# Two cross-attention layers on one core: bias-key fetches, last value weights and one context mix put elsewhere

## The chip, the cores and the metric

The kernel runs on one core of one Trainium2 chip. The metric is the device time of one execution in microseconds (us). The kernel before takes 2015.84 us, the median of three runs (2015.71, 2015.84, 2021.12).

## The reference, cut to what matters

The input is x, 8 batches of 100 rows by 512, and a context ctx of 8 batches of 361 rows by 512. All arithmetic is in 32-bit floats. First comes a small attention with one head (called layer -1 here, its tiles have -1 in their names). Then come two big cross-attention layers l = 0, 1 with 16 heads of 128, and then a two-layer MLP with GELU:

```
h  = layer_norm(x);  q = h @ wq + bq            # per layer
k  = concat(ctx @ wk + bk, bias_k)              # one extra key per head
v  = concat(ctx @ wv + bv, bias_v)              # one extra value per head
x  = x + softmax(q k^T / sqrt(128)) v @ wo + bo
...
x  = x + gelu(layer_norm(x) @ w_fc1 + b_fc1) @ w_fc2 + b_fc2
```

The extra key bias_k needs a score of its own: for each head, a row E = sum over the head of wq * (bias_k - bk) / sqrt(128), which multiplies h. E for layer 1 is what the "bias keys" of this case are about.

## The kernel before, in words

Keys and values are never formed. A head's query is made 512 wide by multiplying with wk (`queries`, tile pq, then `wide_queries`, tile pqw, into the big SBUF array Z). It meets the transposed context cT to give scores (tiles sx, sz, sy, by Winograd's seven products in `pair_part`). The softmax weights are turned by 32x32 transposes on VectorE (`turned`, L358). The weights times ctx give a mixed context (`mixed`, tiles mx, mz, my, back into Z). A head's value weight wv then takes it to the 128 outputs (`head_out`, tile po, into O), and wo follows (`attn_out`, tile pwo).

**Steps and half steps.** A layer is done for four pairs of batches q = 0..3. A pair is done in three groups of rows g = 0..2 (`steps`), and a step has two half steps, one for each batch j of the pair. So a pair has six half steps, k = 2g + j = 0..5. In each half step the score units of that batch (nine or ten groups) are woven with a list `fill` of other units: projections of the next step (`ahead`), mixes of the half step before, head outputs of the step before, products with wo. The order is written out by hand; a list scheduler of the framework then fixes each engine's order from that order and its own estimate of times. Each engine runs its queue in order, and the SP queue, which issues nearly all DMAs, too.

**Closings.** wo is applied for two pairs of batches at once (half hf). Its last ten products, the sum with the rows of x, and the storing of the new rows are the "closing" (`close_units`). For q = 2 it is put into half steps k = 2 and 3 of the same layer; it is closing (0, 0) for layer 0. In k = 3 it fetches four sets of rows xr (`load_rows`, L370), adds to them (`back`, L990), and stores them again (`keep_rows`, L376). Still in k = 3, `rows_unit` fetches the two sets of rows that the next pair (q = 3) needs; they are normalised (L579) and transposed on TensorE (`normed`, ph, L582) at the beginning of k = 4.

**The buffers "h".** Rows fetched by `load_rows` lie in tiles with the tag "h", of which there are two. A fetched pair of bias-key pieces dk (`bias_fetched`, L596) lies in a tile of the same tag.

**The bias keys of layer 1.** There are eight pieces p = 0..7 (two heads each). Each has two units: a fetch (two broadcast DMAs on SP of 128 KB, together with the 512 KB weight tile wqe), and its sums (`bias_keys`: one subtraction on GpSimd, L620, then in `bias_sums` eight multiply-accumulates on VectorE, L603, each with a read of the accumulator; pinned to their place in VectorE's order). All are done in the six half steps of l = 0, q = 2. The fetch is joined to the unit in the middle of `fill`; the sums are put at its end. The pieces by half step k = 0..5 are: 0 / 1 / 2, 3 / 4 / 5 / 6, 7.

**The rings of weights.** `Ring` hands out weight tiles of 512 KB in the order in which units need them: ring "w" has six buffers (wq, wkT, wo, wqe, f1, f2), ring "v" has two (only wv). A new fetch is issued when units have used up earlier tiles.

**The end of layer 1.** For the last pair (l, q) = (1, 3) the head outputs of the first two groups are held back (`held`), and woven into the last step; the rest of them and the outputs of the last group come after the loop, with little score work beside them (`drain`).

**The mix.** In a half step with mixes, `lead` units of `part` (projections and head outputs) come before the first mix. A mix needs sums of columns, made on GpSimd (`column_sums`, L805 to L808) from the turned weights.

Of the kernel before, what the change touches and what calls it, by code (L numbers as in the profile page):

```python
# [19 lines left out]
DT = D // P  # L20
# [13 lines left out]
WHOLE = ((0, 5), (5, 10), (10, 16))  # L34
# [45 lines left out]
def two_cross_attentions(ctx: ExitStack, tc: tile.TileContext, a: dict, out: bass.AP):  # L80
# [11 lines left out]
    def psum(pool, shape, name):  # L92
        return pool.tile(shape, F32, tag=pool.name, name=name)
# [86 lines left out]
    def fill_cT(key, t):  # L180
# [3 lines left out]
    rings = {  # L184
        "ctx": Ring(cpool, [P, 20 * P], "ctx", C_SLOTS, fill_ctx),
        "ctx0": Ring(work, [P, 9 * GWIDTH // 2], "pT", 2, fill_ctx0),
        "cT": Ring(cpool, [P, 7, 2, KH], "cT", C_SLOTS, fill_cT),
        "w": Ring(wpool, [P, 1024], "w", W_SLOTS, fill_w),
        "v": Ring(vpool, [P, 1024], "v", V_SLOTS, fill_w),
    }  # L190
# [13 lines left out]
    def unit(fn, *keys):  # L204
        return fn, keys
# [406 lines left out]
    def bias_fetched(l, p):  # L612
        cols = slice(p * 2 * K, (p + 1) * 2 * K)
        dks[p] = dk = work.tile([P, 2, 2 * K], F32, tag="h", name=f"dk_{l}_{p}")
        broadcast(nc.sync, dk[:, 0, :], l, "bias_k", cols)
        broadcast(nc.sync, dk[:, 1, :], l, "bk", cols)

    def bias_keys(l, p):
        dk = dks.pop(p)
        nc.gpsimd.tensor_tensor(dk[:, 0, :], dk[:, 0, :], dk[:, 1, :], ALU.subtract)  # L620
        bias_sums(l, p, dk[:, 0, :], True)
# [259 lines left out]
            nc.sync.dma_start(out=t[:, j, : (h1 - h0) * L], in_=src.partition_broadcast(P))  # L881
        pbs[l, q] = t, h0

    def head_out(l, q, h):
        w = rings["v"].tiles["wv", l, q, h // 2].rearrange("p (c n) -> p c n", c=DT)
        t, h0 = pbs[l, q]
        add = t[:, :, (h - h0) * L : (h - h0 + 1) * L]
        nc.gpsimd.tensor_scalar(add, add, dv[:, l, h : h + 1], 1.0, ALU.mult, ALU.mult)
        ps = psum(ps_mm, [P, NQ], f"po_{l}_{q}_{h}")
        for c in range(DT):  # L890
            nc.tensor.matmul(  # L891
                ps,
                w[:, c, (h % 2) * K : (h % 2 + 1) * K],
                Z[:, c, :, h * L : (h + 1) * L],
                start=(c == 0),
                stop=(c == DT - 1),
            )
        nc.vector.scalar_tensor_tensor(
            O[:, h // 8, q % 2, h % 8, :].rearrange("p (b t) -> p b t", b=QB),
            ps.rearrange("p (b t) -> p b t", b=QB),  # L900
            vec[f"bv{l + 1}"][:, h : h + 1],
            add,
            ALU.add,
            ALU.add,
        )
# [216 lines left out]
    steps = [(l, q, g) for l in range(2) for q in range(B // QB) for g in range(NG)]  # L1122
# [4 lines left out]
    def e_units(l):  # L1127

        ks = [(W, ("wqe", l, p)) for p in range(H // 2)]
        return [(unit(lambda p=p: bias_fetched(l, p), ks[p]), unit(lambda p=p: bias_keys(l, p), ks[p])) for p in range(H // 2)]  # L1130

    def project_units(n):
        l, q, g = steps[n]
        res = []
        if g == 0:
            res += [unit(lambda c=c: normed(l, q, c)) for c in range(DT)]
            res.append(unit(lambda: bias_scores(l, q)))
        later = None
        h0, h1 = HEADS[g]
        ready = next(h for h in range(H) if (h + 1) * L >= PAIRS[g][0] + 2 * P)  # L1140
        for h in range(h0, h1):
            if q == 0 and h % 2 == 0:
                if later:
                    res += later
                    later = None
                key = "wkT", l, 0, h // 2
                res.append(unit(lambda p=h // 2: wk_transposed(l, p), (W, ("wkr", l, h // 2)), (W, key)))
            res.append(unit(lambda h=h: queries(l, q, h), (W, ("wq", l, q, h // 2))))
            if later:
                res += later  # L1150
            later = [unit(lambda h=h: wide_queries(l, q, h), (W, ("wkT", l, q, h // 2)))]
            if h == ready:
                later.append(unit(lambda: pair_sums(l, q, 0, PAIRS[g][0])))
        return res + later

    def mix_units(n, j):
        l, q, g = steps[n]
        return [
            unit(lambda m=m, part=part: mixed(l, q, g, j, m, part), ("ctx", ("ctx", l, q * QB + j)))
            for m in range(2)  # L1160
            for part in range(4)
        ]

    def out_units(n):
        l, q, g = steps[n]
        res = [unit(lambda h=h: head_out(l, q, h), ("v", ("wv", l, q, h // 2))) for h in range(*WHOLE[g])]
        return [unit(lambda: None)] + res

    def probs_unit(n):
# [22 lines left out]
    def product_units(l, hf, *names):  # L1192
        return [
            unit(lambda cp=cp, name=name: attn_out(l, hf, cp, name), (W, ("wo", l, hf, cp, PRODUCTS[name][0])))
            for name in names
            for cp in range(2)
        ]

    def close_units(l, hf):
        res = [unit(lambda: out_sums(0))]  # L1200
        res += product_units(l, hf, "P3") + [unit(lambda: out_sums(1))] + product_units(l, hf, "P5", "P6", "P7")
        tags = ("h", "h", "hT", "p") if (l, hf) == (1, 1) else ("h",) * 4
        fetch = [unit(lambda b=b, t=t: load_rows(b, t)) for b, t in zip(range(hf * 4, hf * 4 + 4), tags)]
        last = [
            unit(lambda j=j: back(ys[l, hf], j * L, hf * 4 + j, keep_rows)) for j in range(4)
        ]
        if (l, hf) == (1, 1):
            return fetch + res + product_units(l, hf, "P4") + last
        return res + fetch[:2] + product_units(l, hf, "P4") + last[:1] + fetch[2:3] + last[1:2] + fetch[3:] + last[2:]
# [75 lines left out]
    for n, (l, q, g) in enumerate(steps):  # L1285
        ahead = project_units(n + 1) if n + 1 < len(steps) else []
        half_ahead = (len(ahead) + 1) // 2
        for j in range(QB):
            fill = []
            k = 2 * g + j  # L1290
            if q % 2 == 0 and (l or q):
                closing = close_units(*((l, q // 2 - 1) if q else (l - 1, 1)))
                fill += {2: closing[:9], 3: closing[9:]}.get(k, [])
            elif q % 2:
                fill += {(4 if l and q == 3 else 0): product_units(l, q // 2, "P1"), (5 if l and q == 3 else 2): product_units(l, q // 2, "P2")}.get(k, [])
            mix = mix_units(n, 0) if j else mix_units(n - 1, 1) if n else []
            part = ahead[:half_ahead] if j == 0 else ahead[half_ahead:]
            outs = []
            if n == len(steps) - 1:
                outs = held[:4] if j == 0 else held[4:8]  # L1300
            elif j and n:
                outs = out_units(n - 1)
                if n == len(steps) - 2:
                    held, outs = outs + [probs_unit(n)] + out_units(n)[1:], []
            part = woven(part, outs) if len(part) > len(outs) else woven(outs, part)
            if mix:
                lead = (len(part) + 2) // 3 if ahead else len(part) - 2 + j
                fill += part[:lead]
                part = part[lead:]
                fill += woven(part, mix) if len(part) > len(mix) else woven(mix, part)  # L1310
            else:
                fill += part
            if l == 0 and q == 2:
                for fetch, sums_ in e_units(1)[4 * k // 3 : 4 * (k + 1) // 3]:
                    at = len(fill) // 2
                    fill[at] = both_of(fill[at], fetch)
                    fill.append(sums_)
            if l == 0 and q % 2:
                fill = woven(fill, sums_part(q // 2, k))
            if n and j == 0 and n < len(steps) - 1:  # L1320
                (fn, keys), (early, _) = fill[len(fill) * 3 // 4], probs_unit(n - 1)
                fill[len(fill) * 3 // 4] = unit(lambda fn=fn, early=early: [fn(), early()], *keys)
            if g == 1 and j and n < len(steps) - 2:
                at = len(fill) * 3 // 4
                fill[at] = both_of(fill[at], rows_unit((q + 1) % 4))
            groups = score_units(n, j)
            k = 0
            for i, us in enumerate(groups):
                units += us
                upto = (i + 1) * len(fill) // len(groups)  # L1330
                units += fill[k:upto]
                k = upto
    n = len(steps) - 1
# [38 lines left out]
```

## Time and profile before

| | |
|---|---|
| three runs | 2015.71, 2015.84, 2021.12 us |
| the profiled execution | 2018.84 us |
| its span, first to last instruction | 2017.0 us |
| TensorE (PE) busy | 1963.9 us, 97% of the span |
| VectorE (DVE) busy | 1276.8 us, 63% |
| ScalarE (ACT) busy | 757.4 us, 38% |
| GpSimd (POOL) busy | 707.2 us, 35% |
| mean granted TensorE clock | 0.997 |

PE is matmul, PEld the loading of weights into TensorE. A line of the timeline has start, length, engine, line of the kernel, operation, tiles (out<-in), shape and count; the bracket at the end is the engine's idle time just before it and what ended that. Times are from the start of the span.

### The profile page before, as it was taken

Reading aid. Unit: us, or ns where it says so; the run is one execution under the profiler, and the core shown is the slowest. Engines: PE = TensorE matmul, PEld = TensorE weight load, DVE = VectorE, ACT = ScalarE, POOL = GpSimd, SP = SyncE. Lnnn points to the kernel's source line nnn. Section 1 sums busy time; section 2 is a strip of 40 time slices with the busy share of each in tenths; the row PEclk is TensorE's granted clock in tenths of the full one; section 3 lists DMA queues with packets and bytes.
Section 4 is the critical chain, followed back from the end, with each engine's and each line's share of the span. In section 5 each row is a group of like instructions: output and inputs, shape, how many; then the busy total and the mean of one; then the engine's idle time right before and its main releaser. Section 6 shows DMA issues by size and latency. Waiting matters only on the chain.

```text
span 2017.0 us, 31494 instructions
## 1 busy us (share of the span) xinstructions
PE 1963.9 (97%) x10991; PEld 1814.2 (90%) x10991; DVE 1276.8 (63%) x3523; ACT 757.4 (38%) x2002; POOL 707.2 (35%) x1147
## 2 busy tenths in 40 slices
PE   9989999999999999999999999999999999999998
PEld 5668899999999889999999898999998998889998
DVE  2554776667676767666775766676766667765543
ACT  0324544444443343444433344444433444421231
POOL 3223432543345144425243323333243243225140
PEclk9999999999999999999999999999999999999999
DMA  7686224642544446625534453234244442135342
GB/s 252 254 305 218 85 82 141 215 136 76 188 141 138 136 140 207 200 66 176 172 119 128 113 180 102 87 93 158 88 125 125 136 124 79 53 107 168 117 127 73
DMA packets 250682, 283.89 MB, mean 141 GB/s; under 512 B 37608, under 2 KB 212108, under 8 KB 247196
## 3 DMA queue, kind: packets, MB, share of 16 engines
q1 hardware_dynamic: 246340, 271.51, 42.9%
q0 software_dynamic: 2112, 6.40, 0.9%
q10 hardware_dynamic: 2072, 3.97, 0.6%
q8 instruction: 88, 1.44, 0.3%
q14 instruction: 70, 0.57, 0.1%
HBM read 242.86 MB, written 38.97 MB: 140 GB/s over the span
## 4 chain that ended last, share of the span: by engine, by line
PE 79%; DVE 10%; DMA 4%; ACT 3%; issue 2%; POOL 1%; SPq 0%; DVEq 0%; ACTq 0%; POOLq 0%
PE sx L731 9%; PE mx L841 9%; PE mz L841 7%; PE pq L671 7%; PE pqw L687 7%; PE po L891 7%; PE pwo_P L954 6%; DVE pT L358 5%; PE sz L731 5%; PE my L841 3%; PE sc L478 2%; PE sy L731 2%; PE pfx L1094 2%; PE pgx L1045 2%; DMA xr<-xd 1%
## 5 line engine op out<-in xcount | busy, mean ns | idle before, releaser
L358 DVE STREAM_TRANSPOSE pT<-p 32x192 f32<-32x192 f32 (+1 forms) x1664 | 602.1, 362 | 84.3 <-ACT p L342 54.5
L841 PE MATMUL mx<-pT,ctx 128*128 128x256 f32 (+3 forms) x960 | 281.3, 391 | 11.2 <-DVE Z L867 6.6
L731 PE MATMUL sx<-cT,Z 128*128 128x181 f32 x1152 | 229.6, 318 | 3.2 <-DVE p L771 3.1
L841 PE MATMUL mz<-pT,ctx 105*128 105x256 f32 (+3 forms) x768 | 208.3, 393 | 7.3 <-POOL pT L805 4.9
L731 PEld LDWEIGHTS sx<-cT,Z 128*128 128x128 f32 x1152 | 195.2, 191 | 16.6 <-DVE p L771 5.2
L765 POOL TENSOR_SCALAR p<-nsb 128x1 f32<-128x1 f32 x192 | 39.1, 223 | 477.6 <-DVE pT L358 421.4
L841 PEld LDWEIGHTS mx<-pT,ctx 128*128 128x128 f32 (+1 forms) x960 | 170.0, 190 | 30.6 <-DVE Z L867 6.8
L891 PE MATMUL po<-Z,wv 128*128 128x200 f32 x1024 | 194.6, 334 | 1.4 <-DMA wv<-in_L_xattn_wv_dram 1.4
L687 PE MATMUL pqw<-q,wkT 128*128 128x200 f32 x1024 | 194.2, 332 | 0.0
L671 PE MATMUL pq<-hT,wq 128*128 128x200 f32 x1024 | 192.4, 332 | 0.0
L785 ACT ACTIVATE p<-p,nm 128x362 f32<-128x362 f32 x192 | 114.8, 598 | 178.2 <-DVE nm L784 172.5
L891 PEld LDWEIGHTS po<-Z,wv 128*128 128x128 f32 x1024 | 176.4, 191 | 5.6 <-DMA wv<-in_L_xattn_wv_dram 2.0
L841 PEld LDWEIGHTS mz<-pT,ctx 128*128 128x128 f32 (+1 forms) x768 | 144.0, 191 | 40.9 <-ACT Z L853 8.1
L687 PEld LDWEIGHTS pqw<-q,wkT 128*128 128x128 f32 x1024 | 176.2, 189 | 4.8
L671 PEld LDWEIGHTS pq<-hT,wq 128*128 128x128 f32 x1024 | 175.3, 189 | 2.9
L784 DVE TENSOR_REDUCE nm<-p 128x1 f32<-128x362 f32 x192 | 101.6, 529 | 103.6 <-ACT p L776 93.2
L714 POOL TENSOR_TENSOR sums<-Z 128x256 f32<-128x256 f32 x96 | 70.7, 737 | 234.1 <-ACT Z L690 145.4
L690 ACT COPY Z<-pqw 128x400 f32<-128x400 f32 x256 | 122.9, 490 | 73.6 <-PE pqw L687 73.5
L731 PE MATMUL sz<-cT,sums 128*128 128x181 f32 x768 | 149.3, 316 | 0.7 <-ACT p L759 0.7
L342 ACT ACTIVATE p<-p,rden 128x362 f32<-128x362 f32 (+2 forms) x216 | 129.1, 599 | 32.0 <-DVE rden L341 32.0
L731 PEld LDWEIGHTS sz<-cT,sums 128*128 128x128 f32 x768 | 124.8, 189 | 1.0 <-ACT p L759 1.0
L841 PE MATMUL my<-pT,ctx 128*128 128x256 f32 (+3 forms) x384 | 102.5, 388 | 0.0
(380 smaller groups left out, 3123.2 us busy)
## 6 DMA issues: line engine op xcount, KB each, us to landing
wv<-in_L_xattn_wv_dram SPq DMA_DIRECT2D x64, 512.0 KB
wq<-in_L_xattn_wq_dram SPq DMA_DIRECT2D x64, 512.0 KB
wkT<-wkd SPq DMA_DIRECT2D x48, 512.0 KB
cT<-cTd SPq DMA_DIRECT2D x16, 1267.0 KB
wo_S<-wod SPq DMA_DIRECT2D x32, 512.0 KB
f<-in_L_xattn_w_fc_dram SPq DMA_DIRECT2D x32, 512.0 KB
wo_A<-in_L_xattn_wo_dram SPq DMA_DIRECT2D x24, 512.0 KB
xr<-xd SPq DMA_DIRECT2D x45, 200.0 KB
```

Source lines behind the costliest of these rows:

```text
L342: nc.scalar.mul(p[:rows, :n], p[:rows, :n], rden[:rows])
L358: nc.vector.transpose(dst[keys, :, :, i, :], src[i * QD : (i + 1) * QD, :, :, quarter, :])
L671: nc.tensor.matmul(ps, w[:, c, (h % 2) * K : (h % 2 + 1) * K], hTs[l, q][:, c, :], start=(c == 0), stop=(c == DT - 1),)
L687: nc.tensor.matmul(ps[:, c, :], w[:, h % 2, cc * P : (cc + 1) * P], qs[h], start=True, stop=True)
L690: nc.scalar.copy(Z[:, 2 * c2 : 2 * c2 + 2, :, h * L : (h + 1) * L], ps.rearrange("p c (b t) -> p c b t", b=QB),)
L714: nc.gpsimd.tensor_tensor(t[:, 0], a2[:, :2, :], a2[:, 2:, :], ALU.add)
L731: nc.tensor.matmul(ps[:, :KH], st["a"][a][:, c, :], st["ct"][:, blk, c, :], start=(first and c == 0), stop=(c == 1), skip_group_check=not ...
L784: nc.vector.tensor_reduce(nm, p[:, :S1], AX.X, ALU.max, negate=True)
L785: nc.scalar.activation(p[:, :S1], p[:, :S1], AF.Exp, bias=nm, accum_out=den)
L841: nc.tensor.matmul(ps, cx[:w, blk, :], pT[:w, u, :], start=first, stop=last, skip_group_check=more)
L891: nc.tensor.matmul(ps, w[:, c, (h % 2) * K : (h % 2 + 1) * K], Z[:, c, :, h * L : (h + 1) * L], start=(c == 0), stop=(c == DT - 1),)
L954: nc.tensor.matmul(ps, w[:, h, :], OB[i, j][:, h, :], start=(h == 0 and not more), stop=(h == 7), skip_group_check=more)
```

## The change

There are three independent edits.

1. The pieces of the bias keys by half step become 0, 1 / 2, 3 / none / none / 4, 5 / 6, 7. Half steps k = 2 and 3, those with the closing, have none. Each fetch still stands near the middle of `fill`, and each sum at its end.
2. For (l, q) = (1, 3), heads 8 to 15 (four weight tiles wv) take their tile from ring "w" in place of ring "v". In the order of ring "w" these four stand after the last pair's four tiles for products P1 and P2, and before the closing's tiles.
3. In the last step but one, (1, 3, 1), second half step (j = 1), `lead` is larger by one: the mixes begin one unit of `part` later. `part` there is four units: a `pair_sums` (GpSimd), queries of head 15, wide queries of heads 14 and 15. Two stood before the mixes, and one each after four and after eight mixes; now three stand before, and one after all eight.

```diff
-    def head_out(l, q, h):
-        w = rings["v"].tiles["wv", l, q, h // 2].rearrange("p (c n) -> p c n", c=DT)
+    def head_out(l, q, h, ring="v"):
+        w = rings[ring].tiles["wv", l, q, h // 2].rearrange("p (c n) -> p c n", c=DT)
...
     def out_units(n):
         l, q, g = steps[n]
-        res = [unit(lambda h=h: head_out(l, q, h), ("v", ("wv", l, q, h // 2))) for h in range(*WHOLE[g])]
+        def ring(h):
+            return "w" if (l, q) == (1, 3) and h >= 8 else "v"
+
+        res = [
+            unit(lambda h=h: head_out(l, q, h, ring(h)), (ring(h), ("wv", l, q, h // 2))) for h in range(*WHOLE[g])
+        ]
         return [unit(lambda: None)] + res
...
             if mix:
-                lead = (len(part) + 2) // 3 if ahead else len(part) - 2 + j
+                lead = (len(part) + 2) // 3 + (n == len(steps) - 2 and j) if ahead else len(part) - 2 + j
...
             if l == 0 and q == 2:
-                for fetch, sums_ in e_units(1)[4 * k // 3 : 4 * (k + 1) // 3]:
+                for fetch, sums_ in e_units(1)[slice(*{0: (0, 2), 1: (2, 4), 4: (4, 6), 5: (6, 8)}.get(k, (0, 0)))]:
                     at = len(fill) // 2
                     fill[at] = both_of(fill[at], fetch)
                     fill.append(sums_)
```

## The prediction, made before the result was known

> **What bounds the kernel now.** I read the page's first and fourth parts, then TensorE's waits, then a table by stretches around the largest ones, then the timeline.
>
> ```profile
> PE 1963.9 (97%) x10991; PEld 1814.2 (90%) x10991; DVE 1276.8 (63%) x3523; ACT 757.4 (38%) x2002; POOL 707.2 (35%) x1147
> PE 79%; DVE 10%; DMA 4%; ACT 3%; issue 2%; POOL 1%; SPq 0%; DVEq 0%; ACTq 0%; POOLq 0%
> ```
>
> TensorE sets the end. No edit removes work from it, so only its waits can give time. Over the whole span those listed sum to 47.1 us, in 55 waits. Its waits in the half steps of l = 0, q = 2 (560 to 790 us), and then from 1700 to 1850 us:
>
> ```profile
> PE ph L582 <- DVE xr L579: 4.0, 1, 4.0
> PE mx L841 <- DVE Z L867: 2.1, 1, 2.1
> PE sx L731 <- ACT p L756: 1.3, 1, 1.3
> ...
> PE mz L841 <- POOL pT L805: 1.6, 2, 1.0
> PE po L891 <- DMA wv<-in_L_xattn_wv_dram: 1.4, 2, 0.7
> ```
>
> The two largest cost more than they show. Stretches (PE, PEld, DVE, ACT, POOL busy; PE clock; DMA):
>
> ```profile
> 690.05:692.10 2.05, 0.00 (x0) 0.03 (x1) 1.95 (x6) 0.00 (x0) 0.23 (x1) 1.00 0.57 168
> 692.10:696.00 3.90, 3.90 (x12) 3.61 (x13) 3.71 (x10) 0.37 (x1) 1.11 (x3) 0.56 0.31 107
> 708.88:712.86 3.98, 0.01 (x1) 0.00 (x0) 3.18 (x9) 0.37 (x1) 2.02 (x5) 1.00 0.62 204
> 712.86:717.00 4.14, 4.13 (x16) 3.77 (x17) 1.83 (x5) 0.37 (x1) 4.06 (x7) 0.59 0.58 169
> ```
>
> After each wait the clock falls: 3.90 x (1 - 0.56) = 1.72 us and 4.14 x (1 - 0.59) = 1.70 us of matmul time lost. No smaller wait after 150 us has this. So the pair costs 2.06 + 1.72 = 3.78 and 3.98 + 1.70 = 5.68 us, 9.46 together. Why the second is there:
>
> ```profile
> 686.82 0.36 SPq L596 DMA_DIRECT2D dk<-in_L_xattn_bias_k_dram  x1
> 689.52 0.30 SPq L370 DMA_DIRECT2D xr<-xd  x1
> ...
> 708.05 0.80 DVE L603 SCALAR_TENSOR_TENSOR wqe<-wqe,dk 128x128 f32<-128x128 f32 x1
> 708.93 0.31 SPq L370 DMA_DIRECT2D xr<-xd  x1
> 712.27 0.55 DVE L579 TENSOR_SCALAR xr<-xr,mv,rstd 100x512 f32<-100x512 f32 x1 [0.69 <-DVE pT L358]
> 712.87 0.70 PE L582 MATMUL ph<-ident,xr 100*128 100x100 f32 x3 [3.98 <-DVE xr L579]
> ```
>
> The closing frees one "h" buffer at 686.8; piece 4 of the bias keys takes it. The next goes at 689.5 to the first rows of pair q = 3. The second rows must wait until piece 4's last sum ends at 708.85; their fetch goes out at 708.93, and TensorE waits for them.
>
> **What the Trainium skill says.** "TensorE: Matmul & The Clock Gate", Part 1: the clock halves after an idle window of about 3.4 us, a free-running one. The trace agrees on the half and on the length, but shows it after a wait of 2.06 us, so here the trace decides. "SBUF — State Buffer", Who interferes with whom: a VectorE instruction with two SBUF inputs blocks against a GpSimd one that reads SBUF. The trace agrees: one L603 takes 0.28 us mostly, 0.80 at 708.05, while GpSimd runs L717.
>
> **Edit 1, removed.** With no piece in k = 2 and 3, the buffers freed at 686.8 and 689.5 go to the two rows of q = 3. A rows fetch at 680.05 served its reader at 683.08, so they are there by 693, and needed at 708.9. The wait for ph goes, with its clock loss: **-5.68**. VectorE also loses 3.3 us (665.66 to 669.13, pieces 2 and 3) and 3.4 us (piece 4) in these half steps. The other wait, mx on L867, is less sure. VectorE stood 2.72 us for the closing's third rows (683.08) since these await the store of the first ones; that chain stays. The same closings without bias keys, in layer 1, show 2.48 us (q = 0) and 2.56 us (q = 2) of TensorE waits in k = 2 and 3, and no clock loss. Against 9.46 that is 6.9 to 7.0 less. So I take **-1.3** for the second wait, of -3.78 to 0.
>
> **Edit 1, added.** Fetches (two dk DMAs, 0.33 to 0.78 us of SP each, and one wqe) and GpSimd's 0.73 us stay eight each. In k = 1 the fetch of piece 3 stands in SP's queue for a buffer that piece 1's sums free, as piece 2's did at 588.34; in k = 4 the two fetches meet the same release by ph as two do now at 718.56. On VectorE k = 0, 1 and 4 end with 16 sums for 8. Eight took 1.78 us at 741.78. Behind the end of k = 0 stand three transposes, GpSimd's L805 at 588.70 and a mz whose weight load already waits 0.27 us for it: no slack, so 0 to 1.9 us; other projections can stand before it in the new order, and I take **+0.8**. After k = 1 the closing's O-sums (L934) end at 627.9 and are needed at 631.4: 3.5 us of cover hide 1.8. If the cover were gone, 1.8. After k = 4 VectorE's L771 ends at 746.1 for a matmul at 750.2: hidden likewise. The 1.27 us at 786.08, where 16 sums stood ahead of the lone tile's L331, stay: k = 5 has two pieces in both kernels. Two wqe tiles at once leave four of ring "w". The fetches of wqe at 731.80 and 739.87 follow the ends of other tiles' last matmuls (pq at 731.6, pqw at 739.7), so a fetch takes any free buffer, and none waits for a pinned sum with less than 10 us to its use: nothing. Edit 1: -5.68 - 1.3 + 0.8 = **-6.2**.
>
> **Edit 2.** Fetches of wv at 1793.42 and 1814.09, each issued when two heads had ended, met matmuls at 1796.79 and 1817.42: 3.3 us of landing against 2.7 us of two heads.
>
> ```profile
> 1814.09 0.38 SPq L156 DMA_DIRECT2D wv<-in_L_xattn_wv_dram  x1
> 1817.42 1.62 PE L891 MATMUL po<-Z,wv 128*128 128x200 f32 x8 [0.66 <-DMA wv<-in_L_xattn_wv_dram]
> 1801.58 1.13 PE L841 MATMUL mz<-pT,ctx 128*128 128x256 f32 x4 [0.67 <-POOL pT L805]
> ```
>
> In ring "w" the four come out a half step or more ahead: both waits go, 0.66 + 0.70. But behind the first (heads 8, 9) stands mz at 1801.58, waiting for L805; L805 hangs on VectorE's transposes, which did not wait for TensorE there, so its 0.67 grows to 1.37 and that gain is given back. I take **-0.7** of -1.36 to -0.66. Four S1 and S2 tiles of the closing now follow heads 9 to 15. The last is issued about 1820, used about 1834, and lands in 3.3 us: nothing; were it late, some 1 us.
>
> **Edit 3.** At 1714.33 mz waits 0.98 us for L805, and mx 0.25 for L806 next. One wide query (8 matmuls, 1.35 us, as pqw at 1706.24) before them covers both; no DMA moves. It no longer stands after four mixes, where it was cover: **-0.9** of -1.2 to 0.
>
> **Sum:** -6.2 - 0.7 - 0.9 = -7.8. On the profiled execution: span 2017.0 - 7.8 = 2009.2, with its 1.84 around it 2011.0. That execution is 3.0 above the median of the runs; from the median, 2015.84 - 7.8 = **2008.0**.
>
> **Rivals.** (a) The wait moves on: without ph's wait VectorE, 3.18 of 3.98 us busy in it, has no time to catch up, mx on L867 stays with its clock loss, and k = 1 pays its 1.9. For: it ran 9 instructions there. Against: it has 3.4 us less to do just before. -5.68 + 1.9 - 1.6 = -5.4, with half of the ph gain given back -2.5: about 2013. (b) The list order changes after 560 us wherever two instructions were nearly equal, and the waits from there on, 23.2 us without the two large ones, come out otherwise. For: the same half step k = 5 of different pairs shows none or 1.27 us. Against: the units after q = 2 are unchanged. If they grow by a sixth, 3.9, it is 2012; if instead all uncertain terms end at their best, -5.68 - 3.78 - 1.36 - 1.2 = -12.0, 2003.8. (c) Slower: the doubled blocks of sums. At 777.00 a block of 16 took 5.6 us, as GpSimd ran beside it, and stopped L331. If each of the three new ones costs TensorE the 5.6 - 1.8 = 3.8 us and then the clock, 1.7, that is 3 x 5.5 = 16.5, less 5.68 + 1.3 + 1.6: +7.9, about 2024. It decides from about 2 us each, where the clock falls: 3 x 3.7 = 11 against 8.6. Against it: the block of 16 at 665.66 took 3.3 us and no wait followed.
>
> **How the numbers follow.** Forecast 0.66 (own range 2005 to 2011), (a) 0.17, (b) 0.11, (c) 0.06. Two in ten left out gives 2003.5 to 2015. A measurement of this kernel can tell about 0.3%, 6.0 us: faster means below 2009.8. The forecast lies 1.8 under it with about 2 us of spread, so 0.56 of its 0.66 is faster; with 0.05 of (b), 0.61. Slower 0.05 of (c). The rest, 0.34, is the same.
>
> **What would show it.** Right: TensorE's wait for ph gone, no clock loss near 690 to 715; both rows fetches of q = 3 within 3 us of each other; no dk issue in k = 2, 3; no wait of po on wv; mz's wait at the last step but one gone, and a longer one of mz in the drain. Wrong: a new wait of mz or sx at the start of k = 1, a mx wait over 2 us with the clock at half, or a wait on a weight of ring "w".

## The result, and the profile after

The changed kernel takes 2009.66 us, the median of six runs (2007.22 to 2010.5), beside 2017.92 us for the kernel before on the same chip (six runs, 2015.22 to 2021.18). The ratio is 0.9959, with a 95% interval of 0.9947 to 0.9971: 8.3 us less. The profiled execution took 2009.43 us, its span is 2007.7 us; before, 2018.84 and 2017.0.

The page of the kernel after, its first and its fourth part:

```profile
PE 1959.0 (98%) x10991; PEld 1811.7 (90%) x10991; DVE 1277.3 (64%) x3523; ACT 757.0 (38%) x2002; POOL 707.6 (35%) x1147
PE 78%; DVE 12%; ACT 4%; DMA 2%; issue 2%; POOL 1%; SPq 0%; DVEq 0%; ACTq 0%; POOLq 0%
```

The counts of instructions are those of before; TensorE is busy 4.9 us less although it does the same work. That is for the most part the clock: the two falls of before were 3.4 us of it. The waits are 43.0 us in all, where they were 47.1. TensorE's waits of the kernel after, first in the stretch 560 to 790 us, then in 1700 to 1850 us (total, count, longest):

```profile
PE mz L841 <- POOL pT L805: 1.8, 1, 1.8
PE mx L841 <- ACT Z L850: 1.6, 1, 1.6
PE pwo_P L954 <- issue: 1.6, 1, 1.6
PE sx L731 <- ACT p L756: 1.3, 1, 1.3
...
PE mz L841 <- POOL pT L805: 1.6, 1, 1.6
PE mx L841 <- DVE Z L867: 1.4, 1, 1.4
PE sx L731 <- DVE p L771: 1.1, 2, 0.7
```

The 4.0 us of ph and the 2.1 us of mx on L867 are gone. Three waits of 1.6 to 1.8 us stand there that the kernel before did not have. In the second stretch the two waits of po for a DMA are gone, and one wait of mz has grown. In the same stretch as before, the timeline of the kernel after around the rows of the next pair:

```profile
688.45 3.08 SPq L370 DMA_DIRECT2D xr<-xd  x2
...
709.00 0.51 PE L582 MATMUL ph<-ident,xr 100*128 100x100 f32 x4
709.35 0.81 PE L731 MATMUL sx<-cT,sums 128*128 128x181 f32 x4
```

Both rows fetches go out together, 20 us ahead of ph, and ph has no idle time before it. The stretches after the three new waits, in the columns of before (PE, PEld, DVE, ACT, POOL busy; PE clock; DMA):

```profile
591.42:595.40 3.98, 3.98 (x22) 3.71 (x23) 3.29 (x14) 1.87 (x6) 3.98 (x6) 1.00 0.97 295
634.95:639.00 4.05, 4.05 (x24) 4.05 (x25) 2.78 (x10) 1.60 (x4) 2.06 (x3) 1.00 0.90 291
699.57:703.60 4.03, 3.73 (x18) 3.18 (x19) 2.54 (x8) 2.76 (x7) 0.00 (x0) 1.00 0.00 0
```

No clock is lost in these stretches: 1.00 where before had 0.56 and 0.59.

**The two new waits of k = 1.** At its start, in the timeline of the kernel after:

```profile
586.21 0.29 DVE L603 SCALAR_TENSOR_TENSOR wqe<-wqe,dk 128x128 f32<-128x128 f32 x1
...
589.73 0.75 DVE L358 STREAM_TRANSPOSE pT<-p 32x192 f32<-32x192 f32 x2
...
590.57 0.79 POOL L805 TENSOR_TENSOR pT<-pT 128x288 f32<-128x288 f32 x1 [3.80 <-DVE pT L358]
...
591.42 1.24 PE L841 MATMUL mz<-pT,ctx 128*128 128x288 f32 x4 [1.78 <-POOL pT L805]
```

The block of 16 sums stands before the last two transposes; they release GpSimd's L805, and that releases mz. At the end of k = 1:

```profile
617.05 1.83 DVE L930 TENSOR_TENSOR O<-O 128x1600 f32<-128x1600 f32 x1
618.79 5.34 DVE L358 STREAM_TRANSPOSE pT<-p 32x192 f32<-32x192 f32 x14
624.16 1.82 DVE L603 SCALAR_TENSOR_TENSOR wqe<-wqe,dk 128x128 f32<-128x128 f32 x1
...
633.03 1.82 DVE L934 TENSOR_TENSOR O<-O 128x1600 f32<-128x1600 f32 x1
...
622.28 3.56 POOL L932 TENSOR_TENSOR O<-O 128x1600 f32<-128x1600 f32 x1
...
634.95 2.27 PE L954 MATMUL pwo_P<-O,wo_S 128*128 128x200 f32 x12 [1.55 <-issue]
```

The first sum lasts 1.82 us in place of 0.28: it ends at 625.98, just after GpSimd's L932 (625.84). Four more take 0.80 to 0.82 us while GpSimd makes its `pair_sums` (L714 to L717). The block lasts 7.1 us (624.16 to 631.28), L934 follows it and comes too late. "issue" as a releaser means that the profile shows none; L934 ends at 634.85 and the matmul starts at 634.95.

**Where the time went, by stage.** The stage borders are the first sy matmuls of half steps in the timeline: of k = 5 of (l, q) = (0, 1), of (0, 3), of (1, 0), and of k = 3 of (1, 3). Microseconds from border to border, the last one to the end of the span:

| profile of | (0,1) k = 5 and q = 2 | q = 3 | layer 1 up to (1,3) k = 3 | the end |
|---|---|---|---|---|
| before | 265.3 | 196.4 | 726.4 | 304.9 |
| after | 261.7 | 196.1 | 724.2 | 301.7 |
| edit 1 alone | 261.4 | 196.3 | 723.9 | 303.8 |
| edit 2 alone | 264.3 | 196.0 | 725.2 | 303.0 |
| edit 3 alone | 266.7 | 196.4 | 726.5 | 303.3 |
| piece 4 alone moved | 260.3 | 196.3 | 724.3 | 304.6 |
| the same, with idle sums in k = 3 | 264.9 | 196.3 | 726.4 | 304.9 |
| the same, with the buffer held in k = 3 | 265.0 | 196.3 | 724.3 | 305.4 |
| pieces 1, 2, 3 alone earlier | 268.2 | 196.1 | 725.1 | 304.3 |
| piece 4, edits 2 and 3 | 258.8 | 195.8 | 726.3 | 301.8 |
| the same again | 261.0 | 196.1 | 726.3 | 302.3 |
| after again | 261.5 | 196.4 | 724.3 | 301.5 |

Edit 1 acts in the first column (-3.6), edits 2 and 3 in the last (-3.2). In the first column several kernels have the same order of instructions on PE, DVE, ACT and POOL, and so are further executions of one program: before and runs 2 and 3 take 265.3, 264.3 and 266.7 us, the changed kernel, run 1 and the repeat 261.7, 261.4 and 261.5. The difference of the means is 3.9 us.

The -2.2 of layer 1 can't be put down to an edit. From 760 us until edit 3 acts at 1713 us the order of instructions on these four engines is the same before and after. TensorE's waits there sum to 10.2 us before and 8.4 after, in two executions of one order, and the column runs from 723.9 to 726.5 over all these kernels.

### The profile page after: what moved, and what is told of

Its sections match the earlier page's. It is cut to its first block, busy times and chain, and to the rows that moved or that the text cites. A ratio compares the mean times of both kernels' runs of the same rounds, so it can differ in the third digit from the quotient of the medians.

```text
span 2007.7 us, 31493 instructions
## 1 busy us (share of the span) xinstructions
PE 1959.0 (98%) x10991; PEld 1811.7 (90%) x10991; DVE 1277.3 (64%) x3523; ACT 757.0 (38%) x2002; POOL 707.6 (35%) x1147
## 4 chain that ended last, share of the span: by engine, by line
PE 78%; DVE 12%; ACT 4%; DMA 2%; issue 2%; POOL 1%; SPq 0%; DVEq 0%; ACTq 0%; POOLq 0%
PE sx L731 9%; PE mx L841 9%; PE mz L841 7%; PE pq L671 7%; PE po L891 7%; PE pqw L687 7%; PE pwo_P L954 7%; DVE pT L358 6%; PE sz L731 5%; PE my L841 3%; PE sy L731 2%; PE pfx L1094 2%; PE sc L478 2%; PE pgx L1045 2%; ACT p L342 1%
## 5 line engine op out<-in xcount | busy, mean ns | idle before, releaser
L714 POOL TENSOR_TENSOR sums<-Z 128x256 f32<-128x256 f32 x96 | 70.7, 736 | 223.4 <-ACT Z L690 134.8
```

The source lines that it names most:

```text
L714: nc.gpsimd.tensor_tensor(t[:, 0], a2[:, :2, :], a2[:, 2:, :], ALU.add)
```

## The experiments

Each time is against the kernel before on the same chip, as a ratio with its 95% interval; 0.001 is 2.0 us.

**1. The first edit alone.**

```diff
-                for fetch, sums_ in e_units(1)[4 * k // 3 : 4 * (k + 1) // 3]:
+                for fetch, sums_ in e_units(1)[slice(*{0: (0, 2), 1: (2, 4), 4: (4, 6), 5: (6, 8)}.get(k, (0, 0)))]:
```

> Edit 1 alone. Theory A (a piece of bias keys held the buffer that the rows of q = 3 needed; the clock loss goes with the wait): ph's wait and both clock losses gone, mx wait after the closing about 1.6 us as in the closings of layer 1, and the two new waits of the changed kernel (mz on L805 at the start of k = 1, 1.8 us; the third product of the closing in k = 2 on VectorE's L934, 1.6 us) there too: -3.7 us up to the start of q = 3, -4 to -5 in all. Rival B (all of the change's gain is edit 1's, and the rest of the trace's difference chance): -8.

Measured: 0.998 (0.9972 to 0.9987), -4.0 us. Its waits in 560 to 790 us are those of the whole change: mz 1.77, pwo 1.56, mx on L850 1.57, sx 1.3 us, no ph. So edit 1 gave about half of the gain.

**2. The second edit alone** (heads 8 to 15 of the last pair through ring "w").

```diff
+            return "w" if (l, q) == (1, 3) and h >= 8 else "v"
```

> Edit 2 alone. Theory (given back): both waits of po on wv gone (0.70 and 0.66), but the wait of mz on L805 in the drain grows from 0.67 to about 1.4, so -0.7 us. Rival (nothing given back): mz's wait stays at 0.67, -1.4. Rival (ring w now late): a wait of pwo on a weight in the closing, 0 or slower.

Measured: 0.9987 (0.9976 to 0.9997), -2.6 us, and 1.8 us less in the last stage. In its timeline from 1790 to 1822 us one wait of TensorE is left:

```profile
1795.89 1.13 PE L841 MATMUL mz<-pT,ctx 128*128 128x256 f32 x4 [1.65 <-POOL pT L805]
```

Both po waits went, and mz, which stood behind the first, waits 1.65 in place of 0.67 us: a gain of 0.66 + 0.70 is partly given back, as the prediction had it. The order of the matmuls is that of before, so the two traces can be laid over each other, matmul by matmul. The two po bring 0.9 us each, mz takes 0.9 back, and 1.1 us is left at the end of the span. The other 0.7 of the 1.8 us is a wait of sx for L771 at 1774.05 (0.58 us), ahead of all this, which runs 1, 3 and 4, without edit 2, don't have either: it is scatter of the execution before.

**3. The third edit alone.**

```diff
-                lead = (len(part) + 2) // 3 if ahead else len(part) - 2 + j
+                lead = (len(part) + 2) // 3 + (n == len(steps) - 2 and j) if ahead else len(part) - 2 + j
```

> Edit 3 alone. Theory: mz's wait of 0.98 on L805 and mx's 0.25 in (1,3,1) j = 1 gone, a wait of sx on L771 of about 0.7 a few us later in place, as in the changed kernel: -0.5 to -0.8. Rival (full gain): no new wait, -1.2.

Measured: 0.9992 (0.9983 to 1.0001), -1.6 us: no clear difference by itself. In its timeline from 1700 to 1730 us mz's 0.98 and mx's 0.25 are gone, and one wait has come:

```profile
1725.51 0.88 PE L731 MATMUL sx<-cT,Z 128*128 128x181 f32 x4 [0.69 <-DVE p L771]
```

1.23 less 0.69 is 0.5 us of waits. The sums of the three single edits, -4.0 - 2.6 - 1.6 = -8.2 us, agree with -8.3 for the whole, but each has an interval of 1.5 to 2.2 us to either side, so that an agreement within 0.1 us is chance.

**4. Which piece matters: piece 4 alone moved**, from k = 3 to k = 4. Pieces 1 to 3 stay.

```diff
+                for fetch, sums_ in e_units(1)[slice(*{0: (0, 1), 1: (1, 2), 2: (2, 4), 4: (4, 6), 5: (6, 8)}.get(k, (0, 0)))]:
```

> Of edit 1 only piece 4 is moved (pieces 0 / 1 / 2,3 / none / 4,5 / 6,7); k = 0, 1 and 2 as before, edits 2 and 3 not made. Theory A (the buffer): ph's wait with its clock loss gone, no new waits at the starts of k = 1 and in k = 2: at least -5.7 us, and more than edit 1 alone. If the mx wait on L867 in k = 3 came from VectorE's 16 sums at the end of k = 2, it stays (2.1 us and clock loss) and the gain ends at -5.7; if it came from piece 4, it falls to about 1.6 and the gain is about -7.9. Rival (VectorE's relief in k = 2 and 3): a third of the sums moved, -1 to -2.

Measured: 0.9966 (0.9954 to 0.9978), -6.9 us. TensorE's waits in 560 to 790 us:

```profile
PE mx L841 <- DVE Z L867: 2.2, 1, 2.2
PE sx L731 <- ACT p L756: 1.3, 1, 1.3
PE mz L841 <- ACT Z L853: 0.3, 1, 0.3
```

ph's wait is gone, the two of k = 1 do not arise, and mx on L867 stays, with its clock (0.57 in the 3.93 us after it). The whole gain of edit 1 is in this one piece. But piece 4 takes two things out of k = 3: a tile with the tag h, and eight sums from VectorE. The next runs put back one at a time.

**5. Piece 4 moved, and eight idle sums put in its place in k = 3.** They work on zeros and take no tile h.

```diff
+    def idle_sums():
+        zero = ef[:, 2 * DT * H :]
+        for _ in range(8):
+            tc.keep_in_program_order(
+                nc.vector.scalar_tensor_tensor(
+                    zero, zero, 1.0, ident[:, : P - H], ALU.mult, ALU.mult, accum_out=junk_sum
+                )
+            )
...
+            if (l, q, k) == (0, 2, 3):
+                fill.append(unit(idle_sums))
```

> As the run with only piece 4 moved, but with a block of eight idle sums of nearly the same shape (112 columns, zeros times the identity, written back over zeros) left at the end of k = 3 on VectorE, where piece 4's sums stood. Only the buffer is freed, VectorE has the same load there. Theory A (the buffer): ph's wait stays gone, and the time is that of piece 4 alone within 1.5 us: about -6. Rival (VectorE's relief): a wait of ph or of a mix near the start of k = 4 comes back, -2 or less.

Measured: 0.9996 (0.9986 to 1.0005): the gain is gone although the rows are there in time. Lines of this kernel are 11 higher: L816 is L805. Its timeline at the end of k = 3:

```profile
687.99 2.71 SPq L370 DMA_DIRECT2D xr<-xd  x2
...
707.17 0.27 DVE L616 SCALAR_TENSOR_TENSOR E<-E,ident 128x112 f32<-128x112 f32 x1
...
711.87 0.37 DVE L358 STREAM_TRANSPOSE pT<-p 32x192 f32<-32x192 f32 x1
...
712.33 0.81 POOL L816 TENSOR_TENSOR pT<-pT 128x256 f32<-128x256 f32 x1 [0.29 <-DVE pT L358]
...
713.18 1.13 PE L852 MATMUL mz<-pT,ctx 128*128 128x256 f32 x4 [2.34 <-POOL pT L816]
```

Here the sums alternate with the last seven transposes, and these end at 712.24. GpSimd's column sums come after them, and mz after those: 2.34 us, and the clock falls (0.62 over the next 4.02 us). So the sums alone are enough to make TensorE wait, by another chain than the one that the kernel before showed. The order is not quite that of before: there the eight sums stood as a block ahead of the seven transposes.

**6. Piece 4 moved, the tile h held in k = 3 but only one multiply-accumulate.** It was run to see whether the buffer alone would be enough too.

```diff
+    def held_fetch():
+        bias_fetched(1, 4)
+        dks["held"] = dks.pop(4)
+
+    def held_sum():
+        dk = dks.pop("held")
+        half = dk[:, 0, :K]
+        tc.keep_in_program_order(
+            nc.vector.scalar_tensor_tensor(
+                half, half, 1.0, dk[:, 1, :K], ALU.mult, ALU.mult, accum_out=junk_sum
+            )
+        )
...
+            if (l, q, k) == (0, 2, 3):
+                at = len(fill) // 2
+                fill[at] = both_of(fill[at], unit(held_fetch))
+                fill.append(unit(held_sum))
```

> Piece 4 as in the run with piece 4 alone moved (its sums in k = 4); but in k = 3 a tile of the tag h still takes the two rows of bias keys at the old place, and one multiply-accumulate (0.3 us of VectorE) at the old place of the sums lets it go. The output is the reference's. Theory A, the held buffer alone makes TensorE wait: the buffer comes free near 706, the second rows' fetch follows it, 3.9 us from issue to ph as in the kernel before, so ph is ready near 709.9 where it is wanted near 708.5: a wait of 1 to 2 us for ph, none of mz for L805, 2 to 4 us slower than with piece 4 moved. Theory B, the eight sums on VectorE in front of the last transposes alone: nothing of it is seen, the waits of the run with piece 4 moved, -7 us against before. Theory C, the eight sums delay both the release of the buffer and the transposes: the wait for ph is there but short, 0.5 to 2 us, and the 2.34 us of mz seen with idle sums is not; the two runs together give what before showed as one wait.

Measured: 0.9996 (0.9986 to 1.0006), 5.5 us slower than with piece 4 moved. Its timeline:

```profile
705.29 0.31 SPq L370 DMA_DIRECT2D xr<-xd  x1
...
709.01 1.07 DVE L579 TENSOR_SCALAR xr<-xr,mv,rstd 100x512 f32<-100x512 f32 x1 [1.38 <-DMA xr<-xd]
...
710.14 0.59 PE L582 MATMUL ph<-ident,xr 100*128 100x100 f32 x2 [2.95 <-DVE xr L579]
```

The buffer comes free at 704.9, after the one sum, and the second rows are still late: 4.85 us from issue to ph, which is wanted at 707.2. All three theories had the size wrong. A, a wait of 1 to 2 us, is nearest; it is 2.95 us, with a fall of the clock after it. B falls, and so does C's short wait.

Runs 5 and 6 together are the answer to why the kernel before waited. Two chains ended within about a microsecond of each other: buffer, rows, L579, ph; and sums, transposes, L805, mz. In its own trace both are seen:

```profile
708.89 2.69 DVE L358 STREAM_TRANSPOSE pT<-p 32x192 f32<-32x192 f32 x7
711.67 0.72 POOL L805 TENSOR_TENSOR pT<-pT 128x256 f32<-128x256 f32 x1 [0.44 <-DVE pT L358]
713.37 1.96 PE L841 MATMUL mz<-pT,ctx 128*128 128x256 f32 x4
```

L805, which mz needs, ended at 712.39; ph began at 712.87, and mz came right behind it. Only the later chain was listed. Each alone costs nearly all of it (5.6 and 5.5 us over run 4 by the medians, 2016.19 and 2016.13 to 2010.6), and taking either away gains next to nothing. Moving the piece took both away.

**7. The early half of edit 1 alone:** pieces 1, 2 and 3 go to k = 0 and 1, piece 4 stays.

```diff
+                for fetch, sums_ in e_units(1)[slice(*{0: (0, 2), 1: (2, 4), 3: (4, 5), 4: (5, 6), 5: (6, 8)}.get(k, (0, 0)))]:
```

> The other half of the first edit alone: pieces 1, then 2 and 3 go to k = 0 and k = 1 as in the change, piece 4 stays in k = 3. Theory A, the doubled blocks cost what the run with the whole first edit showed over the one with piece 4 alone: a new wait of mz for L805 of about 1.8 us at the start of k = 1 and one of pwo for L934 of about 1.5 us at the end of k = 1, the 3.98 of ph stays: 1 to 3.3 us slower than before, ratio 1.0005 to 1.0016. Rival, the fetches and the closing's chain set the end of k = 3 anyway, so that earlier waits are taken up there: ratio 1.000, the ph wait shorter by what was lost earlier.

Measured: 1.0006 (0.9999 to 1.0013), +1.2 us, and 2.9 us more in the first stage. Its waits in 560 to 790 us:

```profile
PE ph L582 <- DVE xr L579: 4.6, 1, 4.6
PE mz L841 <- POOL pT L805: 1.8, 1, 1.8
PE pwo_P L954 <- issue: 1.5, 1, 1.5
PE mx L841 <- ACT Z L850: 1.4, 1, 1.4
```

Theory A: the two waits of k = 1 belong to the early pieces, and ph's is not shortened but longer. What these pieces bring is a shorter wait in k = 3. In the eight profiles of this document with pieces 2 and 3 in k = 2, the waits of mx and mz from 686 to 702 us sum to 2.1 to 3.8 us (mean 2.8), and five of the eight have a fall of the clock there; in the six profiles without them they sum to 1.7 to 2.1 us (mean 1.9), and none has a fall.

**8. The change without its early half: piece 4 with edits 2 and 3.**

```diff
+                for fetch, sums_ in e_units(1)[slice(*{0: (0, 1), 1: (1, 2), 2: (2, 4), 4: (4, 6), 5: (6, 8)}.get(k, (0, 0)))]:
...
+            return "w" if (l, q) == (1, 3) and h >= 8 else "v"
...
+                lead = (len(part) + 2) // 3 + (n == len(steps) - 2 and j) if ahead else len(part) - 2 + j
```

> Piece 4 alone moved, with edits 2 and 3. If the parts add, the measured ones give -6.9 - 2.6 - 1.6 = -11; by the waits of the traces (ph's 3.98 + 1.7, half or all of 0.70 + 0.66, 1.2 - 0.7) it is -7 to -8. The waits at the starts of k = 1 and in k = 2 that the change brought (1.8 and 1.6 us) are not there, the mx wait of 2.1 us on L867 in k = 3 is, with or without a clock loss. So between equal to the change and 3 us faster than it.

Measured: 0.9956 (0.9945 to 0.9968), 2007.65 us. It was run once more beside the changed kernel, unedited, on one chip:

> Piece 4 alone moved, with the second and third edits: the change without the early half of its first edit. Faster than the changed kernel by 1 to 3 us if the two waits of k = 1 cost what they show; equal if what they cost is taken up by the clock or by later waits.

> The changed kernel beside the next one on the same chip. If the early half of the first edit costs 2 us or more, it is slower than the next one by that; if only the order of instructions differs, equal within 1 us.

Measured: 0.996 (0.9945 to 0.9976), 2009.49 us, and 0.9959 (0.9943 to 0.9975), 2008.89 us. The expected 1 to 3 us between them did not show; all twelve runs of each have medians of 2008.6 and 2009.2 us. The parts did not add up either: runs 2 to 4 give -6.9 - 2.6 - 1.6 = -11.1 us for the first of these, which measured -8.9.

So what does the early half cost? Run 1 against run 4, on one chip, gives 2.2 us by the means (0.8 to 3.6), run 7 1.2 (-0.2 to 2.6), and these twelve runs of each 0.4 (-1.2 to 2.0). All three fit a cost of 0.8 to 2.0 us. Its two new waits are 3.3 us, of which the shorter wait in k = 3 gives back 0.9. Another part seems to be taken up by the clock: its mean is 0.9988 in the twelve runs with the early half and 0.9980 in the twelve without, and 0.0008 of 2009 us is 1.6 us. TensorE's clock after the same wait of mx for L850 (1.57 and 1.56 us), in the changed kernel run again and, second, in this one run again:

```profile
696.30:700.30 4.00, 3.70 (x18) 3.15 (x19) 2.51 (x8) 2.75 (x7) 0.00 (x0) 1.00 0.00 0
...
694.69:698.69 4.00, 3.69 (x11) 2.98 (x12) 2.18 (x7) 1.79 (x6) 0.00 (x0) 0.69 0.00 1
```

The same wait lost clock in one execution and none in the other; the last section shows why.

**9. A wider spread of the pieces**, over q = 1 to 3, at most two to a half step, with edits 2 and 3. It was meant as a faster version.

```diff
-            if l == 0 and q == 2:
-                for fetch, sums_ in e_units(1)[4 * k // 3 : 4 * (k + 1) // 3]:
+            if l == 0:
+                for fetch, sums_ in e_units(1)[slice(*{(1, 4): (0, 1), (2, 0): (1, 2), (2, 1): (2, 3), (2, 4): (3, 5), (2, 5): (5, 6), (3, 0): (6, 7), (3, 1): (7, 8)}.get((q, k), (0, 0)))]:
```

> Edits 2 and 3, and the pieces spread over the neighbouring pairs too, so that no half step before a lone tile or the closing ends with 16 sums: piece 0 in (q = 1, k = 4), 1 and 2 in (2, 0) and (2, 1), 3 and 4 in (2, 4), 5 in (2, 5), 6 and 7 in (3, 0) and (3, 1). If the double blocks cause the waits: against the run before it the mx wait on L867 in k = 3 falls from 2.1 to about 1.6 or less with no clock loss, and the 1.27 at the start of (q = 3, k = 0) goes: 1.5 to 3.5 us faster than it, -10 to -12 against before. If not: the same time as it.

Measured: 0.9993 (0.9983 to 1.0003). The first stage is the shortest of all, 256.4 us, but piece 0 now lies ahead of its border (there mz waits 2.44 us for L805 at 490.36, with a fall of the clock), and q = 3 takes 208.6 in place of 196.4. TensorE's waits there (780 to 985 us), and one instruction of VectorE:

```profile
PE mz L841 <- POOL pT L805: 5.4, 2, 4.4
PE mx L841 <- ACT Z L858: 3.9, 1, 3.9
...
863.20 0.55 DVE L579 TENSOR_SCALAR xr<-xr,mv,rstd 100x512 f32<-100x512 f32 x1 [4.52 <-DMA xr<-xd]
```

The half step with piece 6 ends in 4.4 us of mz on L805. In the one after piece 7, L579 stands at the head of VectorE's queue 4.5 us for rows fetched at 858.82. The two waits and their falls of clock give back more than q = 2 gained.

**10. Run 9 with the O-sum L929 pinned to its place in the last closing.** In the drain it stands on VectorE before the transposes that mz waits for.

```diff
+            ins = nc.vector.tensor_tensor(OB[0, 0], OB[0, 1], OB[0, 0], ALU.subtract)
+            if late:
+                tc.keep_in_program_order(ins)
...
+        res = [unit(lambda: out_sums(0, (l, hf) == (1, 1)))]
```

> As the spread run, and the first of the O-sums (L929) of the last closing is kept behind the last head's output on VectorE. If the L929 beside L805 is what makes L805 2.3 us long in the drain (it is 0.7 elsewhere), mz's wait on L805 there falls from 1.6 us to 0.2 or less: 1.5 us faster than the spread run. If L805 was late for other reasons, the wait stays. If the O-sums are then late for the closing, a pwo wait appears and the gain is gone.

Measured: 1.0004 (0.9995 to 1.0014), no better than run 9. In its timeline L929 went from 1800.70 to 1817.80 and mz's 1.64 us is gone. A wait came instead at wo, behind the moved O-sum (L956 is L954 of the other kernels):

```profile
1817.80 1.81 DVE L929 TENSOR_TENSOR O<-O 128x1600 f32<-128x1600 f32 x1
...
1830.44 9.87 PE L956 MATMUL pwo_P<-O,wo_S 128*128 128x200 f32 x47 [2.06 <-issue]
```

No version here beats the changed kernel by more than its runs scatter.

## Why the prediction was right, and which of its steps were not

The forecast, 2008.0 us and -7.8, stands against 2009.66 and -8.3. The mechanism was right in the main, but that the sum came so near is in part luck: edit 1 brought some 2 us less than forecast (-4.0 for -6.2), the runs of edits 2 and 3 together 2.6 us more (-4.2 for -1.6), and their waits explain only a part of that. In the profiles, 2.2 us of the gain lie in layer 1, where nothing was changed.

- **Edit 1, removed, ph: right in size, half right in cause.** The wait and its clock loss went (5.68), and no clock was lost later. But the prediction put it down to the buffer alone and named VectorE's 3.4 us only in passing. Run 5 shows that freeing the buffer while the sums stay gains nothing that can be measured. A wait in the trace names only the later of two chains; the forecast did not ask what would end next, though its rival (a) did.
- **Edit 1, removed, mx on L867 (-1.3 of -3.78 to 0): about right, as an exchange.** The 2.06 us on L867 became 1.56 on L850, and no fall of the clock came. But the 2.06 was one execution's number: runs 2 and 3, with the same order up to here, wait 1.11 + 1.39 and 2.41 + 1.42 us, both without a fall. The sums under run 7, over all profiles, show the effect of the early pieces better. The closings of layer 1 were the right row to read: that of q = 2 has this same wait of 1.57 us.
- **Edit 1, added, start of k = 1: seen rightly, sized too small.** The wait came at the matmul named, and took 1.78 us, the upper end of 0 to 1.9 where +0.8 was taken. Nothing stood in front of it in the new order. A new wait of mz here was also one of the prediction's own signs of being wrong.
- **"After k = 1 the closing's O-sums (L934) end at 627.9 and are needed at 631.4: 3.5 us of cover hide 1.8": this step failed.** The cover was measured in the order of before, where L930 and L934 stand behind the sums:

```profile
621.69 1.14 DVE L358 STREAM_TRANSPOSE pT<-p 32x192 f32<-32x192 f32 x3
622.86 1.83 DVE L930 TENSOR_TENSOR O<-O 128x1600 f32<-128x1600 f32 x1
...
625.52 2.38 DVE L934 TENSOR_TENSOR O<-O 128x1600 f32<-128x1600 f32 x1
```

 In the new order L930 comes first (617.05) and all the transposes next, so that the block starts 4.3 us later than before (624.16 for 619.87), beside GpSimd. 16 sums took 7.1 us where twice 1.78 was put. It cost 1.55 us of TensorE. The prediction's own rival (c) had the right row, the block of 5.6 us at 777.00, but kept it for the case against. It fell short of (c): waits of 1.78 and 1.55 us, no third, and no fall of the clock. The argument against (c), that no wait followed the block at 665.66, does not hold in view of run 7: with that block the waits in k = 3 are longer. (By its own ends, 665.66 and 669.13, that block took 3.5 us and not 3.3; no sum hangs on it.)
- **Edit 1 in sum:** -6.2 predicted, -3.6 in its stage, -4.0 (-5.7 to -2.6) as a single edit.
- **Edit 2: the mechanism was right to the place.** Both po waits went, and mz in the drain took 0.97 of their 1.36 us back (0.67 to 1.64). By listed waits that is -0.4; matmul by matmul it is -1.1, as a po that waits costs 0.2 us more than its listed wait. The -0.7 lies between. The run alone measured -2.6 (-4.8 to -0.6); what of it goes beyond 1.1 us is not explained and is within its interval.
- **Edit 3: right, too generous in waits.** 0.98 + 0.25 went, 0.69 came on sx for L771, which the prediction did not see: -0.5 for -0.9.
- **Rivals.** (a) has the two chains of the wait almost as runs 5 and 6 found them, "VectorE has no time to catch up", but not that moving the piece also gives VectorE that time. (b) did not come about where it was feared: behind 760 us the order of the four engines changes only from 1713 to 1725 us, where edit 3 acts. But waits come out otherwise even in one order, as layer 1 shows with its 2.2 us.

The Trainium skill, "SBUF — State Buffer", Who interferes with whom, says that a VectorE instruction with two SBUF inputs contends with a GpSimd one that reads SBUF, and that such contention is an exclusive lock. The trace agrees: a sum that otherwise takes 0.28 us starts at 624.16, behind an L932 that began at 622.28, and ends 0.14 us after it, having taken 1.82 us.

## What to carry to other kernels

When a wait is listed under one releaser, look for what else ends just before it: two chains that end together must both be shortened, and an edit that takes away only one gains nothing. Vector work pinned to the end of a stage stands in front of the transposes that start the next stage's matmuls; price it by the slowest block of its kind in the trace, beside GpSimd, not by the mean. Cover that is read off the old order holds only if the new order keeps what stands around it. A wait of one profile is one draw: in one and the same order, that of mx in k = 3 came out between 2.1 and 3.8 us.

## What the runs showed of the hardware

Whether a short wait costs clock seems a matter of chance. In the 14 profiles, from 200 to 2000 us, TensorE has 39 waits of 1.4 to 1.8 us, and 5 of them are followed by a stretch of half clock of 3.4 us. Of 7 waits of 2.0 to 2.5 us, 5 are; of 11 waits of 2.8 us or more, all 11 are, and four of these by 6.8 us.

The traces show what decides it. The starts of half clock in one execution lie whole multiples of 3.413 us apart: in the kernel before, 132.71, 692.50 and 712.98 us are 164 and then 6 of them apart. So the falls come on a grid of windows. It lies differently in each execution: in before and runs 2 and 3, of one order up to there, the falls near 700 us stand 3.0, 0.3 and 2.9 us behind a multiple of 3.413. With this grid laid over the 14 traces, from 200 to 2003 us, 21 windows end in a fall, and TensorE is idle in them for 1.68 to 3.41 us. Of the other windows at full clock, more than 7000, none has over 1.64 us. Here, then, the clock falls after a window that was idle for about half of its length. (Before 200 us four windows idle for 1.66 to 1.85 us have no fall.) Why four stretches last two windows is not shown.

This settles the pair of run 8. In the repeat of run 8, mx's wait of 1.56 us and a wait of 0.30 us of mz, just after it, lie in one window, which is idle for 1.87 us; in the changed kernel run again a border of the grid (697.16) falls between the two, and the first window is idle for only 1.57 us. A wait of 2.41 us in run 3 (to 689.89) is cut by a border at 688.99, and no clock is lost.

The Trainium skill, "TensorE: Matmul & The Clock Gate", Part 1, gives an idle window of about 3.4 us that runs freely. The trace agrees on the length and on running freely; but half of the window is enough here, so the measurement decides.

Such a fall costs 1.7 us, half of 3.41, and much of the scatter between runs goes with it: of 53 runs of the kernel before on one chip, the eight with a mean clock of 0.995 have a median of 2021.05 us, the five with 0.999 one of 2014.28. This difference, 6.8 us, is as large as what the move of piece 4 brings.
